# Layer 0 stores q*v once and gathers the right-hand operand when it is used

## The chip, the cores and the metric

The kernel runs on one core of a Trainium2 chip. The core has five instruction streams: TensorE (PE: matmuls, with weight loads listed as PEld), VectorE (DVE), ScalarE (ACT), GpSimd (POOL) and SyncE (SP). SP, ACT and POOL also issue DMA transfers; the packets of all transfers are moved by the same 16 DMA engines. The metric is the device time of one execution in microseconds; lower is better. A time is the median of several runs.

## The reference, cut to what matters

Four layers run on eight images of 56 x 56 pixels with 192 channels, all in float32: a gated Toeplitz layer (layer 0), window attention, an exponential-average and convolution layer, and a convolution block. The change touches layer 0 alone:

```python
q = silu(x @ q_w.T + q_b)            # 576 channels
v = silu(x @ v_w.T + v_b)
qv = q * v                           # (image, h, w, d)
o1 = toeplitz(qv along w, a1)        # o1[h, w] = sum_w' a1[w - w'] * qv[h, w']
o2 = toeplitz(qv along h, a2)        # o2[h, w] = sum_h' a2[h - h'] * qv[h', w]
out = silu(x @ p_w.T + p_b) * (o1 + o2) @ o_w.T + o_b
```

For each channel d both sums can be had in one matrix product: the left operand holds qv over (h', w) together with a1 as a matrix over (w', w), and the right operand holds a2 as a matrix over (h', h) together with qv over (w', h). The product over the 56 + 56 contraction rows gives o1 + o2 for that channel, 56 x 56 numbers over (w, h).

## The kernel before, in words

**Two steps.** Layer 0 works in two steps, and between them qv lives in DRAM. The first step (the qv step, `layer0_qv`, line 374) computes qv for one image after another; the second (the mix step, `layer0_mix`, line 523) forms the products, gates them, projects them and adds the result to x.

**DRAM tables.** The 576 channels are nine groups of 64 (NSUB = 9). Two DRAM tensors, `left` and `right`, hold rows of QR = 56 x 64 = 3584 floats (14,336 bytes). A row of `left` is one image row h of one image and one channel group: 56 pixels w by 64 channels. A row of `right` is one image column w: 56 pixels h by 64 channels. Behind the images' rows each tensor holds the rows of its Toeplitz matrix, 64 for each channel group: 56 with coefficients and 8 of zeros. `qv_row(b, s)` and `toep_row(s)` give the first row of an image's group and of a group's matrix.

**The qv step.** An image is held as 128 partitions by 1568 pixels: channels of the upper half image in partitions 0 to 63, of the lower half in 64 to 127. A pixel tile is two image rows, 112 pixels, of both halves; there are 14 for each half image (PH). For a tile, TensorE computes q and v for the 112 pixels of each half, 288 channels at a time (line 387); VectorE adds the bias (393), ScalarE applies silu (394), VectorE multiplies q by v (395) into the tile qv, of which there are three buffers. Then SP issues, for each half, one transfer into `left` (line 398) and two into `right` (403), one for each image row. All are packets of 64 floats, 256 bytes. Between tiles, lists of small steps are worked off: the building of the Toeplitz coefficients, their 112 rows and 16 rows of zeros (lines 296 and 301, issued from ACT's queue), the mask of the next layer, and the normalization of the next image, which is called after the fifth tile of the current one.

**The mix step.** Work comes in 72 blocks: eight images by nine channel groups. For a block, `layer0_block` (line 410) loads two tiles of 128 rows, lt and rt, each with one transfer on SP's queue (line 417): even rows from one table part, odd rows from another, so that Toeplitz rows and qv rows alternate and the padding rows (zero Toeplitz rows beside rows of a neighbouring block) add nothing. The pool of these tiles, `raws`, has two buffers for each, so that the load of block n + 2 waits until block n has been copied out. Copies then bring 8 or 16 channels at a time into operand form, lc on POOL and rc in turn on VectorE and ScalarE (line 425), and TensorE multiplies them, one product for each channel (433). Results are copied from PSUM to the tile o (590, 593). There are 40 such rounds an image: eight blocks have four rounds of 16 channels, the ninth has eight rounds of eight. Between rounds, parts of the previous pass's gate (projection, silu, transposes, output projection, lines 445 to 518) are worked off. The copies run two rounds ahead of the products.

**Order.** In layer 0 the framework places instructions on each engine's queue at compile time; each engine then works its queue in order and waits on semaphores. SP's queue is shared by the stores of the qv step, the loads lt and rt, the loads of x (528) and the stores of the result (538). The first two lt loads stand among the stores of the qv step; SP reached them at 400.8 and 431.0 us.

The change alters the source patterns of these loads. Before, a load of lt or rt reads

```python
bass.AP(one.tensor, one.offset, [[QR, 64], [(odd - even) * QR, 2], [1, QR]])
```

a step and a count for each level, the slowest first: 64 rows, for each the Toeplitz and the qv part, then 3584 floats.

Of the kernel before, what the change touches and what calls it, by code (L numbers as in the profile page):

```python
# [10 lines left out]
F32 = mybir.dt.float32  # L11
AF = mybir.ActivationFunctionType
ALU = mybir.AluOpType
# [5 lines left out]
NT = H * W  # L19
# [3 lines left out]
D1 = 576  # L23
# [37 lines left out]


NH = NT // 2
NTH = NH // TT
PH = NPAIR // 2

# [23 lines left out]
def kernel(ctx: ExitStack, tc: tile.TileContext, a: dict, out: bass.AP):  # L90
# [136 lines left out]
    def toeplitz_rows(psum, pool, rows):  # L227
# [145 lines left out]

    def layer0_qv(b, xn, pool, psum, w_qv, b_qv, between):

        lv, rv = (
            z[qv_row(b, 0):qv_row(b, 0) + NSUB * W].rearrange("(s h) (w d) -> s h w d", h=W, d=64) for z in (left, right)
        )
        for i in range(PH):
            qv = pool.tile([2 * W, 2, D1], F32, name="qv", bufs=3)  # L380
            for n in range(2):
                ns = slice(n * D1 // 2, (n + 1) * D1 // 2)
                ps = [psum.tile([2 * W, 2, 512], F32, name=f"qv{s}", tag="qv") for s in range(2)]
                for which in range(2):
                    for j in range(3):
                        for s in range(2):
                            nc.tensor.matmul(  # L387
                                ps[s][:, which, 0:D1 // 2], xn[64 * s:64 * s + 64, j, bass.ts(i, 2 * W)],
                                w_qv[64 * s:64 * s + 64, j, which, ns], start=(j == 0), stop=(j == 2),
                            )  # L390
                for s in range(2):
                    act = pool.tile([2 * W, 2, D1 // 2], F32, name="act", bufs=4)
                    nc.vector.tensor_tensor(act, ps[s][:, :, 0:D1 // 2], b_qv[:, :, ns], ALU.add)  # L393
                    nc.scalar.activation(act, act, AF.Silu)  # L394
                    nc.vector.tensor_tensor(qv[:, s, ns], act[:, 0], act[:, 1], ALU.mult)
            for s in range(2):
                h0 = H // 2 * s + 2 * i
                nc.sync.dma_start(
                    lv[:, h0:h0 + 2].rearrange("s h w d -> (h w) s d"),
                    qv[:, s].rearrange("t (s d) -> t s d", d=64),  # L400
                )
                for r in range(2):
                    nc.sync.dma_start(
                        rv[:, :, h0 + r].rearrange("s w d -> w s d"),
                        qv[r * W:(r + 1) * W, s].rearrange("w (s d) -> w s d", d=64),
                    )
            for step in between[i]:
                step()

    def layer0_block(b, s, raws):  # L410


        raw = [raws.tile([128, QR], F32, name=n) for n in ("lt", "rt")]
        rows_qv, rows_t = qv_row(b, s), toep_row(s)
        for t, z, even, odd in ((raw[0], left, rows_t, rows_qv), (raw[1], right, rows_qv, rows_t)):
            one = z[even:even + 64]
            nc.sync.dma_start(
                t, bass.AP(one.tensor, one.offset, [[QR, 64], [(odd - even) * QR, 2], [1, QR]]),
            )
        return raw  # L420

    def layer0_operand(copy, raw, name, bufs, d0, nu, pool):

        c = pool.tile([128, 2, 8, W], F32, name=name, bufs=bufs)
        copy(c[:, 0:nu], raw.rearrange("p (w u d) -> p u d w", u=nu, d=64 // nu)[:, :, d0:d0 + 8])  # L425
        return c

    def layer0_products(op, nu, lc, rc):
# [893 lines left out]
    with ExitStack() as st:  # L1322
        pool = st.enter_context(tc.tile_pool(reuse_waits="tile", name="qv", bufs=2))
        psum = st.enter_context(tc.tile_pool(reuse_waits="tile", name="qvp", bufs=4, space=PSUM))
        w_qv = resident("w_qv", nc.scalar, pool)
        b_qv = pool.tile([2 * W, 2, D1], F32, name="b_qv", bufs=1)
        nc.scalar.dma_start(b_qv.rearrange("p a d -> p (a d)"), a["b_qv"].partition_broadcast(2 * W))
        tz = st.enter_context(tc.tile_pool(reuse_waits="tile", name="tz", bufs=2))
        x = layer0_load(0, pool)
        xn = layer0_in(0, x, pool, psum)  # L1330
        rows, masks = [], []
        coefs, bias = toeplitz_rows(psum, tz, rows), build_bias_mask(psum, tz, masks)
        centred = layer1_weights(tz, psum)

        def pop(todo, n=1):
            for _ in range(min(n, len(todo))):
                todo.pop(0)()

        for b in range(nimg):

            between = {i: [lambda i=i: pop(rows, 2 if i % 3 == 1 else 1)] for i in range(PH)}
            if b == 0:
                for i in range(PH):
# [340 lines left out]
```

## Time and profile before

| what | us |
|---|---|
| median of three runs | 5754.3 (5746.17 to 5769.35) |
| profiled execution, its own time | 5770.6 |
| its span, first to last instruction | 5768.8 |
| qv step (28.6 to 848) | 819 |
| mix step (848 to 2053) | 1205 |
| the other layers | 3716 |
| TensorE busy in the three stretches | 731, 1084, 3365 |

The profile is of one execution. Matmuls are pipelined, so a busy TensorE is not TensorE at its peak. A group line gives the line of the kernel, the engine, the output and input names, the shape, the count, then busy time and the mean nanoseconds of one, then the idle time of the engine just before such instructions and what ended it. "q1" is the DMA queue that SP fills, "q10" the one that ACT fills; a queue line gives packets, megabytes, and the time that the packets took as a share of 16 engines' time. Where a line of digits stands, it is the busy share of the DMA engines in tenths over 40 equal slices of the window.

### The profile page before, as it was taken

The numbers are of one execution on the slowest core, as the hardware profiler recorded it, in microseconds if no ns is written. First come the engines' busy times: TensorE is split into PE (matmuls) and PEld (weight loads), VectorE is DVE, ScalarE is ACT, GpSimd is POOL, SyncE is SP. The second block draws the span as 40 slices with busy tenths as digits, with TensorE's granted clock in tenths as the row PEclk, the third lists the DMA queues.
The fourth block names the chain that finished last, engine by engine and source line by source line (L and its number), as shares of the span: only waits on it lengthen the run. The fifth ranks groups of instructions, "written<-read, shape, count | busy, mean of one in ns | idle before, by whom it ended". The sixth has DMA issues, their size and how long they took to land. (4 is left out here: it accounts for less than half of the span.)

```text
span 5768.8 us, 116138 instructions
## 1 busy us (share of the span) xinstructions
PE 5181.2 (90%) x50342; PEld 3376.1 (59%) x50342; DVE 3336.5 (58%) x4710; ACT 2169.1 (38%) x2908; POOL 1420.2 (25%) x1107
## 2 busy tenths in 40 slices
PE   6898998999899979999997989999788798999999
PEld 4568765666666645555554657676344597444444
DVE  5777774555555546566665868888778202433331
ACT  2333443333333423333332004555476400433333
POOL 2100004444444424433342013333101101100100
PEclk8999999999999989999998989999899899999999
DMA  6888986776677633222222866666687598212211
GB/s 179 204 211 216 206 182 258 264 264 258 247 262 264 222 92 82 69 75 76 69 65 76 260 235 218 227 232 209 160 232 215 222 328 295 78 62 77 76 41 26
DMA packets 721922, 1013.94 MB, mean 176 GB/s; under 512 B 486376, under 2 KB 645444, under 8 KB 694644
## 3 DMA queue, kind: packets, MB, share of 16 engines
q1 hardware_dynamic: 706352, 940.12, 52.4%
q0 software_dynamic: 8512, 40.62, 2.1%
q10 hardware_dynamic: 6548, 25.78, 1.4%
q8 instruction: 396, 6.49, 0.5%
q14 instruction: 114, 0.93, 0.0%
HBM read 676.92 MB, written 345.97 MB: 177 GB/s over the span
## 5 line engine op out<-in xcount | busy, mean ns | idle before, releaser
L387 PE MATMUL qv<-w_qv_sb,xn 64*112 64x288 f32 x5376 | 711.3, 421 | 48.6 <-DVE act L393 45.4
L425 POOL COPY lc<-lt 128x896 f32<-128x896 f32 (+1 forms) x320 | 552.5, 1751 | 640.9 <-PE op L433 543.1
L387 PEld LDWEIGHTS qv<-w_qv_sb,xn 64*112 64x112 f32 x5376 | 558.5, 182 | 195.5 <-DVE act L393 58.1
L394 ACT ACTIVATE act<-act 112x576 f32<-112x576 f32 x448 | 300.6, 683 | 466.8 <-DVE act L393 427.4
L433 PE MATMUL op<-rc,lc 128*56 128x56 f32 x9216 | 339.1, 221 | 102.1 <-POOL lc L425 64.9
L433 PEld LDWEIGHTS op<-rc,lc 128*56 128x56 f32 x9216 | 307.8, 135 | 177.9 <-POOL lc L425 103.5
L1289 PE MATMUL ph<-y,w_sb 64*128 64x392 f32 x2304 | 397.7, 497 | 6.5 <-ACT hid L1293 6.5
L1300 PE MATMUL po<-hid,w_sb 128*64 128x392 f32 x2304 | 386.3, 494 | 0.0
L393 DVE TENSOR_TENSOR act<-qv,b_qv 112x576 f32<-112x576 f32 x448 | 320.7, 752 | 92.7 <-PE qv L387 92.4
L1307 DVE TENSOR_TENSOR x<-x,z 128x392 f32<-128x392 f32 x96 | 67.0, 698 | 524.2 <-ACT z L1305 524.2
L425 ACT COPY rc<-rt 128x896 f32<-128x896 f32 (+1 forms) x160 | 256.3, 1606 | 249.7 <-PE op L433 227.2
L805 PE MATMUL qk_ps<-xr,wg 64*96 64x392 f32 x1536 | 334.2, 538 | 1.8 <-DVE xr L752 1.7
L1016 PE MATMUL cv<-zc,wt 128*128 128x224 f32 x1536 | 313.6, 356 | 24.2 <-DMA zc<-pd 24.2
L1016 PEld LDWEIGHTS cv<-zc,wt 128*128 128x128 f32 x1536 | 291.0, 190 | 67.5 <-issue 51.2
L1289 PEld LDWEIGHTS ph<-y,w_sb 64*128 64x128 f32 x2304 | 220.0, 188 | 175.9 <-issue 25.5
L445 PE MATMUL pj<-xn,w_p_sb 64*128 64x392 f32 x1536 | 309.8, 511 | 12.4 <-DVE xn L533 8.2
L1190 PE MATMUL cps<-zc,wt 128*128 128x224 f32 x1536 | 300.2, 356 | 18.2 <-DMA zc<-zd 16.8
L1190 PEld LDWEIGHTS cps<-zc,wt 128*128 128x128 f32 x1536 | 289.6, 189 | 28.7 <-issue 21.3
L466 PE MATMUL y<-pp,w_o_sb 128*64 128x392 f32 x1536 | 285.9, 501 | 4.8 <-DVE x L474 4.1
L459 DVE TENSOR_TENSOR pp<-pp,ot 128x784 f32<-128x784 f32 x128 | 124.2, 970 | 284.8 <-ACT pp L450 272.9
L1300 PEld LDWEIGHTS po<-hid,w_sb 128*64 128x64 f32 x2304 | 162.7, 137 | 213.8 <-issue 213.8
L1031 POOL TENSOR_TENSOR rows<-rows,loc 128x896 f32<-128x896 f32 x96 | 220.8, 2300 | 261.7 <-ACT rows L1027 201.9
(233 smaller groups left out, 8895.1 us busy)
## 6 DMA issues: line engine op xcount, KB each, us to landing
lt<-left SPq DMA_DIRECT2D x72, 1792.0 KB
rt<-right SPq DMA_DIRECT2D x72, 1792.0 KB
left<-qv SPq DMA_DIRECT2D x224, 252.0 KB
right<-qv SPq DMA_DIRECT2D x448, 126.0 KB
wt<-in_band_dram SPq DMA_DIRECT2D x23, 2048.0 KB
wt<-in_band_dram SPq DMA_DIRECT2D x11, 4096.0 KB
zc<-pd SPq DMA_DIRECT2D x187, 232.0 KB
pd<-pt SPq DMA_DIRECT2D x7, 5568.0 KB
```

What stands on the lines that cost most here:

```text
L387: nc.tensor.matmul(ps[s][:, which, 0:D1 // 2], xn[64 * s:64 * s + 64, j, bass.ts(i, 2 * W)], w_qv[64 * s:64 * s + 64, j, which, ns], start ...
L393: nc.vector.tensor_tensor(act, ps[s][:, :, 0:D1 // 2], b_qv[:, :, ns], ALU.add)
L394: nc.scalar.activation(act, act, AF.Silu)
L425: copy(c[:, 0:nu], raw.rearrange("p (w u d) -> p u d w", u=nu, d=64 // nu)[:, :, d0:d0 + 8])
L433: nc.tensor.matmul(op[64 * u:64 * u + W, i, :], lc[:, u, i], rc[:, u, i], start=True, stop=True)
L445: nc.tensor.matmul(ps[0:M, s, 0:TT], w_p[64 * s:64 * s + 64, j, d0:d0 + M], xn[64 * s:64 * s + 64, j, ts], start=(j == 0), stop=(j == 2),)
L466: nc.tensor.matmul(y[64 * s:64 * s + 64], w_o[0:M, c, 64 * j:64 * j + 64], pp[0:M, s], start=(c == gated[0][0]), stop=(c == gated[-1][0]),)
L805: nc.tensor.matmul(in_pairs(ps[s]), wg[64 * s:64 * s + 64, j, c0:c0 + HC], in_slots(xr[64 * s:64 * s + 64], (3 * g + j) * GW), start=(j == ...
L1016: nc.tensor.matmul(dst, wt[:, c4 + i, 128 * q:128 * q + 128], zc[:, :, c4 + i, q:q + NPAIR], start=(q == 0), stop=(q == 1),)
L1190: nc.tensor.matmul(dst.rearrange("p (b n) -> p b n", n=NPAIR), wt[:, c4 + i, q * OP:(q + 1) * OP], zc[:, :, c4 + i, q:q + NPAIR], start=(q ...
L1289: nc.tensor.matmul(ps[:, s, 0:TT], w0[64 * s:64 * s + 64, j, m * 128:(m + 1) * 128], y[64 * s:64 * s + 64, j, ts], start=(j == 0), stop=(j ...
L1300: nc.tensor.matmul(ps[64 * s:64 * s + 64], w1[:, m, 64 * j:64 * j + 64], hid[:, m, s], start=(m == 0), stop=(m == 5),)
```

## The change

Pixel tiles are now cut without regard to image rows: twelve of 120 pixels and one of 128 for each half image, 13 in place of 14 (QT). qv is stored once, to `left`, one transfer for each half; the stores to the images' rows of `right` are gone, and `right` holds the Toeplitz rows alone. The right-hand operand's qv half is gathered in the mix step out of the rows of `left`: for each column w, 56 packets of 64 floats. The rows of zeros are gone and a block has 112 rows, the first 56 of one part and the last 56 of the other. For lt this is one transfer whose source pattern lists the two parts first, then the 56 rows; for rt there are two transfers. The operand tiles lc and rc have 112 rows.

```diff
+QT = [(120 * i, 120) for i in range(12)] + [(1440, 128)]
...
-    none = dram.tile([QR], F32, name="none")
-    left, right = (dram.tile([(nimg * W + 64) * NSUB, QR], F32, name=n) for n in ("left", "right"))
+    left, right = (dram.tile([n * NSUB, QR], F32, name=z) for n, z in ((nimg * W + 64, "left"), (64, "right")))
...
-        zero = pool.tile([128, QR // 128], F32, name="zero", bufs=1)
-        nc.gpsimd.memset(zero, 0.0)
-        nc.scalar.dma_start(none.rearrange("(p n) -> p n", p=128), zero)
-        parts = [z[toep_row(0):].rearrange("(s k) n -> k s n", k=64) for z in (left, right)]
+        parts = [z[at:].rearrange("(s k) n -> k s n", k=64) for z, at in ((left, toep_row(0)), (right, 0))]
...
-        def zeros(i, k):
-            nc.scalar.dma_start(parts[i][k], none.partition_broadcast(NSUB))
-
-        rows += [lambda i=i, k=k: zeros(i, k) for i in range(2) for k in range(W, 64)]
...
     def layer0_qv(b, xn, pool, psum, w_qv, b_qv, between):
-        lv, rv = (
-            z[qv_row(b, 0):qv_row(b, 0) + NSUB * W].rearrange("(s h) (w d) -> s h w d", h=W, d=64) for z in (left, right)
-        )
-        for i in range(PH):
-            qv = pool.tile([2 * W, 2, D1], F32, name="qv", bufs=3)
+        one = left[qv_row(b, 0):qv_row(b, 0) + NSUB * W]
+        for i, (t0, M) in enumerate(QT):
+            qv = pool.tile([128, 2, D1], F32, name="qv", bufs=3)
...
-                                ps[s][:, which, 0:D1 // 2], xn[64 * s:64 * s + 64, j, bass.ts(i, 2 * W)],
+                                ps[s][0:M, which, 0:D1 // 2], xn[64 * s:64 * s + 64, j, t0:t0 + M],
...
             for s in range(2):
-                h0 = H // 2 * s + 2 * i
                 nc.sync.dma_start(
-                    lv[:, h0:h0 + 2].rearrange("s h w d -> (h w) s d"),
-                    qv[:, s].rearrange("t (s d) -> t s d", d=64),
+                    bass.AP(one.tensor, one.offset + 64 * (NH * s + t0), [[64, M], [64 * NT, NSUB], [1, 64]]),
+                    qv[0:M, s].rearrange("t (s d) -> t s d", d=64),
                 )
-                for r in range(2):
-                    nc.sync.dma_start(
-                        rv[:, :, h0 + r].rearrange("s w d -> w s d"),
-                        qv[r * W:(r + 1) * W, s].rearrange("w (s d) -> w s d", d=64),
-                    )
...
     def layer0_block(b, s, raws):
         raw = [raws.tile([128, QR], F32, name=n) for n in ("lt", "rt")]
-        rows_qv, rows_t = qv_row(b, s), toep_row(s)
-        for t, z, even, odd in ((raw[0], left, rows_t, rows_qv), (raw[1], right, rows_qv, rows_t)):
-            one = z[even:even + 64]
-            nc.sync.dma_start(
-                t, bass.AP(one.tensor, one.offset, [[QR, 64], [(odd - even) * QR, 2], [1, QR]]),
-            )
+        x = left[qv_row(b, s):qv_row(b, s) + W]
+        nc.sync.dma_start(
+            raw[0][0:2 * W], bass.AP(x.tensor, x.offset, [[(toep_row(s) - qv_row(b, s)) * QR, 2], [QR, W], [1, QR]])
+        )
+        nc.sync.dma_start(raw[1][0:W], right[64 * s:64 * s + W])
+        nc.sync.dma_start(
+            raw[1][W:2 * W].rearrange("w (h d) -> w h d", d=64), x.rearrange("h (w d) -> w h d", d=64)
+        )
         return raw

     def layer0_operand(copy, raw, name, bufs, d0, nu, pool):
-        c = pool.tile([128, 2, 8, W], F32, name=name, bufs=bufs)
-        copy(c[:, 0:nu], raw.rearrange("p (w u d) -> p u d w", u=nu, d=64 // nu)[:, :, d0:d0 + 8])
+        c = pool.tile([2 * W, 2, 8, W], F32, name=name, bufs=bufs)
+        copy(c[:, 0:nu], raw[0:2 * W].rearrange("p (w u d) -> p u d w", u=nu, d=64 // nu)[:, :, d0:d0 + 8])
         return c
...
-            between = {i: [lambda i=i: pop(rows, 2 if i % 3 == 1 else 1)] for i in range(PH)}
+            between = {i: [lambda i=i: pop(rows, 2 if i % 3 == 1 else 1)] for i in range(len(QT))}
```

Left out are the bias, activation and product lines of `layer0_qv`, which take the first M rows of their tiles, the bias tile `b_qv`, which has 128 rows in place of 112, and the loop that works off the coefficient steps, which runs over the 13 tiles.

More of the change, by code (lines that the diff above doesn't have):

```diff
@@ L374, in layer0_qv @@
     def layer0_qv(b, xn, pool, psum, w_qv, b_qv, between):
-        lv, rv = (
-            z[qv_row(b, 0):qv_row(b, 0) + NSUB * W].rearrange("(s h) (w d) -> s h w d", h=W, d=64) for z in (left, right)
-        )
-        for i in range(PH):
-            qv = pool.tile([2 * W, 2, D1], F32, name="qv", bufs=3)
+        one = left[qv_row(b, 0):qv_row(b, 0) + NSUB * W]
+        for i, (t0, M) in enumerate(QT):
+            qv = pool.tile([128, 2, D1], F32, name="qv", bufs=3)
             for n in range(2):
                 ns = slice(n * D1 // 2, (n + 1) * D1 // 2)
-                ps = [psum.tile([2 * W, 2, 512], F32, name=f"qv{s}", tag="qv") for s in range(2)]
+                ps = [psum.tile([128, 2, 512], F32, name=f"qv{s}", tag="qv") for s in range(2)]
                 for which in range(2):
@@ L391, in layer0_qv @@
                 for s in range(2):
[L392 to L395, printed above, removed]
+                    act = pool.tile([128, 2, D1 // 2], F32, name="act", bufs=4)
+                    nc.vector.tensor_tensor(act[0:M], ps[s][0:M, :, 0:D1 // 2], b_qv[0:M, :, ns], ALU.add)
+                    nc.scalar.activation(act[0:M], act[0:M], AF.Silu)
+                    nc.vector.tensor_tensor(qv[0:M, s, ns], act[0:M, 0], act[0:M, 1], ALU.mult)
             for s in range(2):
-                h0 = H // 2 * s + 2 * i
                 nc.sync.dma_start(
-                    lv[:, h0:h0 + 2].rearrange("s h w d -> (h w) s d"),
-                    qv[:, s].rearrange("t (s d) -> t s d", d=64),
-                )
-                for r in range(2):
-                    nc.sync.dma_start(
-                        rv[:, :, h0 + r].rearrange("s w d -> w s d"),
-                        qv[r * W:(r + 1) * W, s].rearrange("w (s d) -> w s d", d=64),
-                    )
+                    bass.AP(one.tensor, one.offset + 64 * (NH * s + t0), [[64, M], [64 * NT, NSUB], [1, 64]]),
+                    qv[0:M, s].rearrange("t (s d) -> t s d", d=64),
+                )
             for step in between[i]:
@@ L1325 @@
         w_qv = resident("w_qv", nc.scalar, pool)
-        b_qv = pool.tile([2 * W, 2, D1], F32, name="b_qv", bufs=1)
-        nc.scalar.dma_start(b_qv.rearrange("p a d -> p (a d)"), a["b_qv"].partition_broadcast(2 * W))
+        b_qv = pool.tile([128, 2, D1], F32, name="b_qv", bufs=1)
+        nc.scalar.dma_start(b_qv.rearrange("p a d -> p (a d)"), a["b_qv"].partition_broadcast(128))
         tz = st.enter_context(tc.tile_pool(reuse_waits="tile", name="tz", bufs=2))
@@ L1339 @@
         for b in range(nimg):
-            between = {i: [lambda i=i: pop(rows, 2 if i % 3 == 1 else 1)] for i in range(PH)}
+            between = {i: [lambda i=i: pop(rows, 2 if i % 3 == 1 else 1)] for i in range(len(QT))}
             if b == 0:
-                for i in range(PH):
+                for i in range(len(QT)):
                     between[i].insert(0, lambda: [next(coefs, None) for _ in range(2)])
```

## The prediction, made before the result was known

> **What bounds the kernel now.** I read the page first, for who is busy and how often the lines of the diff run.
>
> ```profile
> PE 5181.2 (90%) x50342; PEld 3376.1 (59%) x50342; DVE 3336.5 (58%) x4710; ACT 2169.1 (38%) x2908; POOL 1420.2 (25%) x1107
> ...
> L387 PE MATMUL qv<-w_qv_sb,xn 64*112 64x288 f32 x5376 | 711.3, 421 | 48.6 <-DVE act L393 45.4
> ...
> lt<-left SPq DMA_DIRECT2D x72, 1792.0 KB
> ```
>
> TensorE is the busy engine overall, but only layer 0 is touched, so the stretches come next: the qv step, the mix step, the untouched rest, and one steady stretch of qv.
>
> ```profile
> 28.60:848.00 819.40, 731.27 (x5514) 574.94 (x5514) 598.94 (x1124) 320.40 (x469) 42.88 (x76) 0.93 0.85 197
> 848.00:2053.00 1205.00, 1084.20 (x14932) 728.82 (x14932) 652.41 (x817) 470.02 (x467) 556.12 (x326) 0.97 0.67 249
> 2053.00:5768.80 3715.80, 3364.51 (x29896) 2071.34 (x29892) 2073.62 (x2734) 1377.18 (x1972) 811.04 (x682) 0.96 0.47 147
> ...
> 750.00:825.00 75.00, 75.00 (x622) 55.69 (x620) 60.29 (x104) 34.37 (x52) 0.00 (x0) 1.00 0.88 180
> ```
>
> The columns after the length are PE, PEld, DVE, ACT and POOL busy, granted clock, DMA share, GB/s. Undisturbed, qv is paced by TensorE (75.00 of 75 us). In the mix step TensorE is busy 1084 of 1205 us; DMA is not the pace over the whole (0.67). What the loads cost now is in the view of tile lt, and where they run in the DMA view of one image's last block.
>
> ```profile
> L425 POOL COPY lc<-lt x320: 944/1763/2862, 848.5 to 2040.9; 128x896 f32<-128x896 f32 x128, 128x448 f32<-128x448 f32 x32
> ...
>   DMA lt<-left: 62.7, 14
> ```
>
> ```profile
> DMA  5096999999950000000000000000000000979990
> ...
> q1 hardware_dynamic: 464, 5.73, 36.6%
> ```
>
> POOL waited for lt only 62.7 us in 14 places. In the second view (1700 to 1740) the engines run full for a dozen us, then idle until a buffer comes free: loads come in bursts over all engines, with slack. Last, how a transfer spreads. The packet records show one 4-byte packet per engine at the end of each transfer, so these count engines. While the Toeplitz rows are written:
>
> ```profile
> q10 hardware_dynamic: 991, 7.10, 8.6%
> ...
> left<-coef ACTq DMA_DIRECT2D x55, 126.0 KB
> ```
>
> 55 transfers of nine 14,336-byte rows are 495 packets; the other 496 are nine closings each: nine engines, not 16. The packet records give 3 engines for coef<-ct (111 outer rows). On SP's queue they hold 28,000 closings for 1,806 transfers: exactly 16 for each whose outer count is 64, 112 or 128, and 14 for each of the 448 right<-qv with 56. The count always divides the outer count.
>
> **The change part by part.**
>
> *Thirteen tiles for fourteen.* A tile is 48 matmul records (5376/112); 75 us/622 is 0.1206 us each, 5.8 us a tile. Eight tiles fewer: -46 us, on the path since TensorE paces. DVE, its cover, needs 4 x (0.752 + 0.461) = 4.9 us a tile and stays under. A weight load of 120 columns lies between 0.182 us (112, this line) and 0.188 us (128, L1289), both under a pair of matmuls; zero, at worst 2496 x 0.006 = 15 us if exposed.
>
> *Stores.* 448 SP issues of right<-qv and their 58 MB go; 224 of left<-qv become 208. Steady qv runs at DMA 0.88 with TensorE full, so nothing is waited for there; ACT's waits for left<-qv (12.2 us) are the upper bound. I take 0. The 16 zero rows on ACT's queue (0.69 us each, 11 us in image 0, where ACT is mostly idle) also go: 0, at best -11.
>
> *lt, 112 rows.* The destination still has 112 outer rows, but the source pattern now begins with the pair [.., 2], then 56 rows; before it began with 64, then the pair. If the engines divide the outer index on both sides, two engines carry everything: 56 rows each. The median packet of 14,336 bytes takes 0.535 us in the packet records: 56 x 0.535 = 30.0 us a block, where 128/16 x 0.535 = 4.3 us do now. The trace has no transfer with unequal counts below 16, so the other end is a spread by the destination's 112: 3.75 us. I take two engines: the nearest rows, 9, 56 and 111, all lost engines to their outer count, and a slice by the outer index of both sides can't be finer than 2.
>
> [...]
>
> *rt, in two pieces.* The Toeplitz half, 56 rows: 14 engines, four packets each, 4 x 0.535 = 2.1 us. The gather is 56 x 56 packets of 256 bytes, 224 on each of 14 engines. Nearest row, the same size in the other direction:
>
> ```profile
> q1 hardware_dynamic: 71655, 17.96, 87.6%
> ```
>
> 0.876 x 16 x 100 us / 71,655 = 0.0196 us a packet (725 to 825): 4.4 us. Ends: 15 ns (shortest 196-byte mask read in the packet records) gives 3.4 us, 46 ns (their median) 10.3 us.
>
> [...]
>
> *Mix step.* If the two engines also carry their share of rt, each block holds them 30.0 + 2.1 + 4.4 = 36.5 us, against 1205/72 = 16.7 us a block now. raws has two buffers: the load of block n+2 is issued when block n is copied out, at most some 19 us after it landed in the first eight blocks of an image, so a load is always queued and the ring runs on. From the third block, 70 x 36.5 = 2555. Each image's x load and two stores ride the same rings: 8 packets x 0.70 us and 24 of 6,272 bytes, about 0.24 us each: 11 x 8 = 90. The ninth block is held from 1702.4 to 1740.1 in POOL's timeline, 38 us, so the ring waits some 3.5 us: 25 for seven. Together 2670 us. Now these 70 take from the issue at 862.4 to about 1996 (the last lt is issued at 1986.3, ten us before it lands): 1134. Difference +1536. What follows the last load is the same. SP sees three issues per block for two and waits in order; it is otherwise empty there. Queued behind lt on these rings are rt and x, counted above.
>
> POOL, DVE and ACT copies are priced by the free size and keep 896 elements (112 rows for 128): 0. Matmuls keep 56 columns: 0. The cover that hid the loads, the gate work between the products, is gone at 30 us a load.
>
> *The first two lt inside qv.* SP issues them at 400.8 and 431.0, between stores. Stores behind them share the two rings.
>
> ```profile
> 425.00:450.00 25.00, 16.94 (x122) 13.44 (x122) 12.76 (x26) 8.03 (x11) 0.54 (x1) 0.90 0.99 296
> ```
>
> There TensorE already loses 8 us to one. At 30 us, less two spare qv tiles of 5.8, the loss is 18: +10 each, +20; between 0 and +44 (nothing spare).
>
> **Sum.** -46 + 20 + 1536 = +1510 us. On the profiled execution's 5770.6 that is 7281; it stood 16 above the median of 5754.3, so I predict 7265.
>
> **The rivals.**
>
> *A, lt spreads over 16 engines and the kernel is faster.* Engines 1 to 14 then carry 3.75 + 2.1 + 4.4 = 10.3 us a block, against 256/16 x 0.535 = 8.6 now and 16.7 of work. The waits for lt (62.7) grow by some 10 to 20 and the tiles give -46: about 5720, -0.6%. It decides from where a block's load fits in 16.7 us: lt on seven engines or more (112/7 x 0.535 = 8.6, plus 6.5). For it: destination 112 would allow 16. Against: the counts above.
>
> *B, lt on two engines, the pieces of rt on others.* The trace names no engine per packet. Then a block is 30.0: 70 x 6.5 = 455 less, 6810.
>
> *C, dear gather.* At 46 ns the block is 42.4: +5.9 x 70 = 413, 7680. With lt spread out it would be 16.2 us, about +5 on the eight blocks that now take some 11 us each: 5754 - 46 + 320 = 6030.
>
> **How the numbers follow.** The likeliest, two engines with rt behind lt, 0.77; B 0.08; C 0.07 with two engines and 0.02 with lt spread; A 0.06. The likeliest alone: packets at 0.586 us (1700 to 1740: 0.366 x 16 x 40 us / 400 large packets) give +3.1 x 70 = +215, and 15 ns in the gather gives -70: 7190 to 7490. The range takes in B and C: 6790 to 7690. 0.5%, about 29 us, is what a measurement of this kernel can tell (three runs spread over 23). Of A, 0.05 is faster and 0.01 within 0.5%; the other cases are slower, 0.94.
>
> **What would show it.** Right: in the mix step a DMA share near 0.28, GB/s near 95, POOL or the rc copies waiting for lt or rt about 20 us a block, lt<-left and rt<-right leading the waits, and 1,152 large lt packets fewer (16 x 72, the padding rows). The qv step: 4992 matmuls and about 790 us. Wrong: a mix step near 1205 with POOL's wait for lt under 100 us (A), waits that end on rt alone (C), or blocks 30 us apart (B). The prediction falls if lt's closings are 16 a transfer.

## The result, and the profile after

The changed kernel takes 7600.9 us (four runs, 7597.9 to 7604.6) against 5761.8 for the kernel before: 1.3195 times as long, 95% interval 1.3159 to 1.3231. Its profiled span is 7599.8 us against 5768.8. By stretches; the mix step runs from the start of the first lc copy to the start of the last o copy:

| stretch, us | before | after |
|---|---|---|
| qv step, up to the first copy | 848.5 | 834.3 |
| mix step | 1204.3 | 3051.6 |
| the other layers | 3716.0 | 3713.8 |

From the page of the changed kernel, the busy times and the costliest groups of layer 0:

```profile
PE 5418.5 (71%) x49958; PEld 3515.4 (46%) x49958; DVE 3253.4 (43%) x4646; ACT 2143.1 (28%) x2876; POOL 1367.5 (18%) x1106
...
L420 PE MATMUL op<-rc,lc 112*56 112x56 f32 x9216 | 460.6, 274 | 1437.9 <-DVE rc L412 1371.1
...
L412 POOL COPY lc<-lt 112x896 f32<-112x896 f32 (+1 forms) x320 | 499.7, 1583 | 2541.0 <-DMA lt<-left 1936.9
L412 DVE COPY rc<-rt 112x896 f32<-112x896 f32 (+1 forms) x160 | 140.1, 910 | 1676.2 <-DMA rt<-left 1660.6
...
L378 PE MATMUL qv<-w_qv_sb,xn 64*120 64x288 f32 (+1 forms) x4992 | 668.0, 425 | 37.2 <-DVE act L384 33.8
```

TensorE was 90% busy and is 71% busy. The products wait 1371 us for VectorE's copies to rc, those copies wait 1661 us for rt, and POOL waits 1937 us for lt: behind all three stand loads. The windows of the three stretches (length, then PE, PEld, DVE, ACT and POOL busy, granted clock, DMA share, GB/s):

```profile
28.60:834.00 805.40, 687.38 (x5122) 539.27 (x5120) 560.03 (x1058) 298.25 (x436) 39.14 (x71) 0.90 0.52 126
834.00:3886.00 3052.00, 1362.74 (x14930) 901.25 (x14932) 598.42 (x817) 466.05 (x467) 503.17 (x326) 0.67 0.38 88
3886.00:7599.80 3713.80, 3364.84 (x29896) 2072.18 (x29892) 2081.16 (x2734) 1375.95 (x1972) 812.25 (x682) 0.96 0.47 147
```

All of the loss lies in the mix step, where the DMA engines move 88 GB/s in place of 249 and are 0.38 busy: slow and mostly idle at once. The view of tile lt (issues with least, median and longest duration in ns; then what POOL waited for, us and times):

```profile
L400 SPq DMA_DIRECT2D lt<-left x72: 615/31996/48967, 372.9 to 3783.1; - x72
...
  DMA lt<-left: 1936.9, 70
```

and the DMA view of 18 us in which only an lt load is under way:

```profile
DMA  1211011111001111001111001111101111101111
...
q1 hardware_dynamic: 68, 0.97, 12.8%
```

12.8% is two engines of 16. The 4-byte closing packets, one for each engine that carries a transfer, say the same: SP's queue has 21,136 in the changed kernel, which comes out exactly with two for each lt, 14 for each piece of rt, 15 for a store of 120 rows and 16 for one of 128, all other transfers as in the kernel before. The issue of such a load took SP 0.5 us before; its median is now 32 us, about as long as the load moves. SP's own timeline over one block:

```profile
903.20 32.18 SPq L400 DMA_DIRECT2D lt<-left  x1
935.57 0.88 SPq L403 DMA_DIRECT2D rt<-right  x1
936.50 0.38 SPq L404 DMA_DIRECT2D rt<-left  x1
944.49 31.60 SPq L400 DMA_DIRECT2D lt<-left  x1
```

The rt loads go out only after lt's issue has ended, and the next lt follows 41.3 us after the one before. What the rt loads do when they come is in the DMA view of 936 to 948:

```profile
DMA  2009115999469948548999999999999999957122
...
q1 hardware_dynamic: 2846, 1.79, 84.3%
```

Twelve engines that had nothing to do move their shares of rt in one burst of some ten us, and then idle again.

### The profile page after: what moved, and what is told of

Same layout as the page of the kernel before. It is cut to its first block, busy times and chain, and to the rows that moved or that the text cites. A ratio compares the mean times of both kernels' runs of the same rounds, so it can differ in the third digit from the quotient of the medians.

```text
span 7599.8 us, 114683 instructions
## 1 busy us (share of the span) xinstructions
PE 5418.5 (71%) x49958; PEld 3515.4 (46%) x49958; DVE 3253.4 (43%) x4646; ACT 2143.1 (28%) x2876; POOL 1367.5 (18%) x1106
## 5 line engine op out<-in xcount | busy, mean ns | idle before, releaser
L420 PE MATMUL op<-rc,lc 112*56 112x56 f32 x9216 | 460.6, 274 | 1437.9 <-DVE rc L412 1371.1
L420 PEld LDWEIGHTS op<-rc,lc 112*56 112x56 f32 x9216 | 427.0, 185 | 1509.7 <-issue 1438.9
L412 POOL COPY lc<-lt 112x896 f32<-112x896 f32 (+1 forms) x320 | 499.7, 1583 | 2541.0 <-DMA lt<-left 1936.9
L412 ACT COPY rc<-rt 112x896 f32<-112x896 f32 (+1 forms) x160 | 254.6, 1591 | 1828.6 <-DMA rt<-left 1698.5
L378 PE MATMUL qv<-w_qv_sb,xn 64*120 64x288 f32 (+1 forms) x4992 | 668.0, 425 | 37.2 <-DVE act L384 33.8
L378 PEld LDWEIGHTS qv<-w_qv_sb,xn 64*120 64x120 f32 (+1 forms) x4992 | 523.4, 192 | 175.8 <-DVE act L384 45.5
L385 ACT ACTIVATE act<-act 120x576 f32<-120x576 f32 (+1 forms) x416 | 279.6, 683 | 470.4 <-DVE act L384 432.4
L384 DVE TENSOR_TENSOR act<-qv,b_qv 120x576 f32<-120x576 f32 (+1 forms) x416 | 297.6, 751 | 96.7 <-PE qv L378 96.6
L432 PEld LDWEIGHTS pj<-xn,w_p_sb 64*128 64x128 f32 x1536 | 172.0, 206 | 349.2 <-ACT pp L437 217.5
L1021 DVE TENSOR_TENSOR_SCAN sums<-dec,rows 64x896 f32<-64x896 f32 x96 | 279.3, 2910 | 1.3
```

Source lines behind the costliest of these rows:

```text
L378: nc.tensor.matmul(ps[s][0:M, which, 0:D1 // 2], xn[64 * s:64 * s + 64, j, t0:t0 + M], w_qv[64 * s:64 * s + 64, j, which, ns], start=(j == ...
L384: nc.vector.tensor_tensor(act[0:M], ps[s][0:M, :, 0:D1 // 2], b_qv[0:M, :, ns], ALU.add)
L385: nc.scalar.activation(act[0:M], act[0:M], AF.Silu)
L412: copy(c[:, 0:nu], raw[0:2 * W].rearrange("p (w u d) -> p u d w", u=nu, d=64 // nu)[:, :, d0:d0 + 8])
L420: nc.tensor.matmul(op[64 * u:64 * u + W, i, :], lc[:, u, i], rc[:, u, i], start=True, stop=True)
L432: nc.tensor.matmul(ps[0:M, s, 0:TT], w_p[64 * s:64 * s + 64, j, d0:d0 + M], xn[64 * s:64 * s + 64, j, ts], start=(j == 0), stop=(j == 2),)
```

## The experiments

Each is compared with runs of the kernel before on the same chip. "Large packet" is a row of 14,336 bytes, "small" one of 256 bytes; their times are means over the packet records of the mix step (median where said); the small packets of the stores and of the copies inside DRAM are those of the qv step.

| kernel | time, us | ratio to before, 95% | mix step, us | large packet, us | small, ns |
|---|---|---|---|---|---|
| before | 5754 to 5765 | 1 | 1204.3 | 0.584 (median 0.535) | 19.6 (stores) |
| after | 7600.9 | 1.3159 to 1.3231 | 3051.6 | 0.746 | 32 |
| lt as two transfers | 6115.0 | 1.0580 to 1.0625 | 1638.6 | 1.027 | 33 |
| lt on three engines | 6835.2 | one run | 2339.0 | 0.821 | 31 |
| before, lt on two engines | 7905.8 | one run | 3282.2 | 0.842 | - |
| no gather | 6039.2 | 1.0456 to 1.0494 | 1539.0 | 1.008 | - |
| before, in halves | 6120.2 | 1.0592 to 1.0648 | 1544.5 | 1.070 | - |
| halves on two queues | 6230.4 | 1.0771 to 1.0837 | 1734.2 | 1.002 and 0.942 | 31 |
| 112 rows, alternating | 6064.8 | 1.0501 to 1.0542 | 1557.5 | 1.015 | 32 |
| 128 rows, gather | 5958.6 | 1.0342 to 1.0373 | 1459.3 | 0.604 (median 0.535) | 22 |
| before, program order | 5852.5 | 1.0143 to 1.0175 | 1301.3 | 0.570 (median 0.535) | - |
| 128 rows, gather, program order | 5831.9 | 1.0106 to 1.0136 | 1349.3 | 0.605 (median 0.535) | 22 |
| lt as two transfers, program order | 6121.7 | 1.0602 to 1.0637 | 1643.6 | 1.028 | 33 |
| right copied inside DRAM | 5738.3 | 0.9943 to 0.9976 | 1241.9 | 0.583 (median 0.535) | 18 |

**Is it the two engines?** The theory of the prediction: lt's source pattern begins with a level of two, so two engines carry the whole block. Three kernels test it: take the level away, put it into the kernel before, and change two into three.

```diff
-        nc.sync.dma_start(
-            raw[0][0:2 * W], bass.AP(x.tensor, x.offset, [[(toep_row(s) - qv_row(b, s)) * QR, 2], [QR, W], [1, QR]])
-        )
+        nc.sync.dma_start(raw[0][0:W], x)
+        nc.sync.dma_start(raw[0][W:2 * W], left[toep_row(s):toep_row(s) + W])
```

> The changed kernel with lt loaded by two transfers of 56 rows (outer count 56 on both sides, as the two parts of rt) in place of one with outer count 2. Theory (two engines carry lt): 8 packets of 0.54 us on each of 14 engines instead of 56 on each of two; lt, rt and the gather then hold an engine for about 11 us a block, under the 16.7 us of work, so the mix step comes back from 3052 us to 1205 to 1270 and the whole to 5700 to 5800 us. Rival (the gather of 256-byte packets is what costs): lt is a small part, the mix step stays over 2500 us and the whole over 7000.

The same for the kernel before, the other way round:

```diff
-        for t, z, even, odd in ((raw[0], left, rows_t, rows_qv), (raw[1], right, rows_qv, rows_t)):
...
+        nc.sync.dma_start(
+            raw[0], bass.AP(one.tensor, one.offset, [[(rows_t - rows_qv) * QR, 2], [QR, 64], [1, QR]]),
+        )
+        for r, at in ((0, rows_t), (64, rows_qv)):
+            nc.sync.dma_start(raw[1][r:r + 64], right[at:at + 64])
```

> The kernel before with lt loaded by one transfer whose source lists the two parts first and then 64 rows (outer count 2), rt by two transfers of 64 rows; 14 pixel tiles, both stores and the zero rows as before, no gather. Theory: 64 packets of 0.54 us on two engines are 34.6 us, with rt's eight packets 39 us a block; mix step about 70 x 39 + 115 = 2845 and the whole 7350 to 7550 us, though nothing else of the change is in it. Rival (the gather or the 112 rows cost it): near the kernel before, 5740 to 5850 us.

And three engines, by cutting each half of lt into 51 rows (three divides 51) and five:

```diff
+        for r, at in ((0, qv_row(b, s)), (W, toep_row(s))):
+            nc.sync.dma_start(raw[0][r:r + 51], left[at:at + 51])
+            nc.sync.dma_start(raw[0][r + 51:r + W], left[at + 51:at + W])
```

> The changed kernel with each half of lt loaded as 51 rows and 5 rows. If an engine count must divide the outer count (51 = 3 x 17, 5), three engines carry nearly all: 2 x (17 + 1) = 36 packets, 19.5 us, with rt 2.2 and the gather 4.4 a block of 26 us, plus about 2 where rt's burst meets it: mix step 2000 to 2250, whole 6450 to 6800 us. Rival (any split into two or more transfers cures it, because it was the unequal shapes of the two sides that cost): the same as with two transfers of 56 rows, 5700 to 5800 us.

Measured: 6115 us without the level of two, 7906 us with it in the kernel before, which has no gather and all its stores, and 6835 us with three engines. All three lie above the ranges given in advance, by 315, 356 and 35 us. The DMA view of a stretch of lt in the kernel before with that pattern (3002 to 3050):

```profile
DMA  1111111111111111111111111111111111111111
...
q1 hardware_dynamic: 186, 2.57, 12.6%
```

and of the kernel with three engines (1500 to 1700):

```profile
DMA  6988999411289311289511279621269712168912
...
q1 hardware_dynamic: 20508, 23.67, 54.2%
```

The closing packets on SP's queue come out exactly with 14 engines for each half of lt in the first kernel (23,008 in all), two for lt in the second (28,144), and three and five for its pieces in the third (22,144). The two-engine pattern is enough for the loss: the second kernel's rt also comes in halves, but the kernel before with both tiles in halves, further down, takes 6120 us. One engine more gives back 713 of 3052 us of the mix step. The cause is shown from both sides. But without it the kernel is still 6% behind the kernel before, where the prediction's rival A had put a spread load at 5720.

**What holds the other 6%? First the gather.** In the kernel with lt as two transfers, the gather is replaced by a contiguous load of the same 56 rows; the exchange of rows and columns is left out.

```diff
-        nc.sync.dma_start(
-            raw[1][W:2 * W].rearrange("w (h d) -> w h d", d=64), x.rearrange("h (w d) -> w h d", d=64)
-        )
+        nc.sync.dma_start(raw[1][W:2 * W], x)
```

> The kernel with lt in two transfers of 56 rows, and the gather of 256-byte packets replaced by a load of the same 56 rows as they lie, 14,336 bytes a packet: it leaves out the exchange of rows and columns in the right-hand qv, so it computes another sum; same bytes, same work elsewhere. Theory: the gather costs an engine 4.4 to 9 us a block where the large packets cost 2.2, but the blocks have slack, so the whole is 0 to 60 us under the kernel with the gather. Rival (the gather is the bottleneck once lt is spread): more than 150 us under it.

6039 us against 6115: without the 3136 small packets a block the kernel is 76 us faster, a fifth of what is missing, and TensorE's order of work, of which more below, differs between the two as well. The large packets still take 1.008 us where the kernel before has 0.584, so the transfers themselves are slow.

**Then where the rows land.** The kernel before, its tables, stores and 14 tiles as they were, loads lt and rt as two halves, rows for partitions 0 to 63 and for 64 to 127, in place of alternating rows:

```diff
-            nc.sync.dma_start(
-                t, bass.AP(one.tensor, one.offset, [[QR, 64], [(odd - even) * QR, 2], [1, QR]]),
-            )
+            nc.sync.dma_start(t[0:64], z[first:first + 64])
+            nc.sync.dma_start(t[64:128], z[second:second + 64])
```

> The kernel before with lt and rt each loaded by two transfers of 64 rows to partitions 0 to 63 and 64 to 127, in place of one transfer of 64 x 2 rows to all 128; same bytes, same 16 engines by outer count, no gather, 14 pixel tiles. Theory (a transfer to half of the partitions runs at half the rate: in the last runs its 14,336-byte packets took 1.0 to 1.1 us where those of the 128-row transfers took 0.54): 16 packets of 1.07 us, 17 us a block where 8.6 were, mix step 1205 to some 1550, whole 6050 to 6200 us. Rival (the 56 rows or the 14 engines cost it): packets stay at 0.54 us and the whole at 5740 to 5800.

6120 us, large packets a median of 1.104 us, about twice 0.535: the same rows, bytes and engines (64 rows on 16 engines), in half of the partitions at a time, at half the rate. Two queues might have let the two halves overlap:

```diff
-        nc.sync.dma_start(raw[0][W:2 * W], left[toep_row(s):toep_row(s) + W])
+        nc.scalar.dma_start(raw[0][W:2 * W], left[toep_row(s):toep_row(s) + W])
...
-        nc.sync.dma_start(
+        nc.scalar.dma_start(
             raw[1][W:2 * W].rearrange("w (h d) -> w h d", d=64), x.rearrange("h (w d) -> w h d", d=64)
```

> The kernel with lt in two transfers of 56 rows (6115 us), with the second half of lt and the gather issued from ACT's queue, so that transfers to the lower and the upper partitions are under way together. Theory (each half of the partitions has its own limit, and one queue serves the halves one after the other): large packets come down toward 0.54 us, a block toward 11 to 14 us, whole 5690 to 5850 us. Rival (the rate is lost by splitting as such, or ACT's waits for buffers cost as much as is won): 6000 us or more, packets still at 1.0 us.

They did not: 0.94 to 1.00 us a packet, and 6230 us in all. ACT, which had copies of rc to do, now spent 164 us of the mix step on issues (22.3 us on one lt half), and the rc copies waited 632 us for the gather, against 304 with one queue; which of the two made the loss is not shown. Next, the changed kernel's parts in alternating partitions, lt again as one transfer with the 56 rows as the outer level:

```diff
-            raw[0][0:2 * W], bass.AP(x.tensor, x.offset, [[(toep_row(s) - qv_row(b, s)) * QR, 2], [QR, W], [1, QR]])
+            raw[0][0:2 * W], bass.AP(x.tensor, x.offset, [[QR, W], [(toep_row(s) - qv_row(b, s)) * QR, 2], [1, QR]])
...
+        even, odd = raw[1][0:2 * W].rearrange("(k r) n -> r k n", r=2)[0], raw[1][0:2 * W].rearrange("(k r) n -> r k n", r=2)[1]
+        nc.sync.dma_start(even, right[64 * s:64 * s + W])
+        nc.sync.dma_start(odd.rearrange("w (h d) -> w h d", d=64), x.rearrange("h (w d) -> w h d", d=64))
```

> The changed kernel with the two parts of lt and rt in alternate partitions: lt by one transfer whose source lists 56 rows first and then the two parts (outer counts 56 and 112: 14 engines), the Toeplitz half of rt to the even and the gather to the odd partitions, so every transfer touches lower and upper partitions. Theory (half of the partitions, half the rate): the halves are no longer served one after the other, packets under 1.0 us, whole 5720 to 6000 us. Rival (the split to 14 engines with neighbouring rows on one engine is what costs, wherever the rows go): packets stay at 1.0 to 1.1 us and the whole at 6050 to 6150.

6065 us, large packets still 1.015 us, and 1.02 where no small packet is near. And the same with the padding rows given back, 64 rows a part, so that every transfer has 16 engines:

```diff
+        nc.sync.dma_start(raw[0], bass.AP(x.tensor, x.offset, [[QR, 64], [far * QR, 2], [1, QR]]))
+        even, odd = (raw[1].rearrange("(k r) n -> r k n", r=2)[r] for r in range(2))
+        nc.sync.dma_start(even, right[64 * s:64 * s + 64])
+        nc.sync.dma_start(
+            odd.rearrange("w (h d) -> w h d", d=64), bass.AP(x.tensor, x.offset, [[64, 64], [QR, W], [1, 64]])
+        )
```

> The changed kernel with blocks of 128 rows again and its two parts in alternate partitions: lt by one transfer of 64 x 2 rows as before, the Toeplitz half of rt (64 rows, zero rows restored) to the even and the gather (64 columns, the last 8 unused) to the odd partitions; 13 pixel tiles, qv stored once. Differs from the interleaved 112-row kernel (6065 us) in 64 rows for 56. Theory (transfers whose rows divide by 64 give each engine its own part of the partitions; 56 rows make engines meet, whichever partitions they go to): large packets back at 0.54 to 0.6 us, 256-byte packets near 20 ns, a block 4.3 + 2.1 + 4.3 = 10.7 us, mix step 1205 to 1280; with the qv step 60 us shorter than before the whole is 5680 to 5780 us. Rival (it is splitting rt into a part and a gather, or loading alternate partitions, that costs): packets stay at 1.0 us and 31 ns, the whole at 6000 to 6100.

The packets are back at a median of 0.535 us and 22 ns, and 14% more bytes take 98 us less of the mix step than 112 alternating rows do. The whole still missed its range (5680 to 5780) by 179 us. So the half rate was measured in two ways: with half of the partitions (in halves, a median of 1.104 us) and with 56 rows a part on 14 engines, even over nearly all partitions (1.044). Why 14 engines cost as much as half the partitions, these runs don't say: from the alternating kernel to this one the rows, the engines and the partitions change together, and the packet records name no engine, so that engines meeting at the destination, the theory above, is argued and not shown. It is a rate of many engines at once: in the changed kernel the two engines that come last carry the same 56-row pieces at 0.538 us a row and 15.8 ns a small packet.

**The rest of it is order.** With its packets back at that rate the 128-row kernel still has a mix step of 1459 us, 255 above the kernel before, and POOL hardly waits for loads. From the view of its tile lt, what POOL waited for:

```profile
  PE op L427: 913.2, 112
  DMA lt<-left: 1.4, 3
```

Here TensorE holds the copies up. The framework had placed the gate's work elsewhere: the order in which TensorE works one image's mix step (the fourth) is, with the number of matmuls in a row (op: products; pj, ot, y: gate), from the trace:

```
before               ... op96 pj12 ot1 op32 ot13 op32 pj12 ot14 op31 y1 op1 y23 op32 pj12 ot14 ...
128 rows, gather     ... pj10 op128 pj26 op128 ot28 y16 ot2 y8 ot11 pj1 ot1 pj11 ot14 y16 pj2 y2 op128 ...
the same, pr. order  ... op32 pj12 ot14 op32 pj12 ot14 op32 y24 op64 pj12 ot14 op32 pj12 ot14 op32 y24 ...
```

In the second the gate comes in lumps, and the products eight rounds at a time (elsewhere in this image sixteen); while a lump of gate work runs, the buffers of lc and rc don't come free. That the loads alone can change the order is shown by the kernel before in halves, which differs from the kernel before in nothing else. The changed kernel, the kernel before in halves and both alternating kernels share this bunched order (all but four of 14,929 records agree). Lt as two transfers has a third order, in longer lumps, with up to 24 rounds of products in a row. To take the order out of the comparison, three kernels keep the mix step's instructions on TensorE, VectorE and ScalarE as the code issues them; POOL's order was the same in all. Their sequences are then identical from the first product to the last.

```diff
         psum = st.enter_context(tc.tile_pool(reuse_waits="tile", name="mixp", bufs=2, space=PSUM))
+        st.enter_context(tc.manual_schedule(engines=IN_ORDER))
```

> The kernel before, with the instructions of TensorE, VectorE and ScalarE in the mix step kept in the order in which the code issues them; nothing else is changed. It is the control for the next two runs, which have exactly this order on all four engines, and so differ from it by their loads and by the 13 tiles alone. What the written order itself costs is unknown: the gate pieces stand between the rounds as the lists of the code have them, which is the even spread, so the mix step should lie between 1204 us (nothing lost) and 1459 us (the bunched order of the 128-row gather kernel). Total 5750 to 6020.

> The 128-row kernel with the gather (lt as one transfer, rt as 64 Toeplitz rows to even and the gather to odd partitions), with the same fixed order of instructions in the mix step as the control. Theory order: that kernel's mix step of 1459 us against 1204 comes from gate work that the compiler bunched; with the order fixed its mix step is within 40 us of the control's, and the total is 20 to 60 us below the control's (the 13 tiles). Theory transfers: a third transfer a block and 3584 small packets cost the 217 to 255 us themselves, whatever the order; then its mix step is over 200 us above the control's.

> The changed kernel with lt as two 56-row transfers (large packets at 1.03 us, 256-byte packets at 33 ns), in the same fixed order. A block then holds each of 14 engines 8 x 1.03 + 4 x 1.03 + 224 x 0.033 = 19.8 us, against 16.7 us of work a block in the kernel before: 72 x 19.8 = 1426, less the early blocks and with the x loads about 1430 to 1500. Theory half rate: the mix step stays 1430 to 1640, 150 us or more above the 128-row kernel in the same order. Theory order: packets are slow but hidden, and its mix step is within 50 us of the 128-row kernel's.

The windows of the three mix steps, first the control (the kernel before's loads), then the 128-row gather, then lt as two transfers:

```profile
848.00:2149.00 1301.00, 1085.31 (x14926) 749.06 (x14927) 606.25 (x817) 460.94 (x466) 595.25 (x325) 0.91 0.61 230
```

```profile
782.00:2131.00 1349.00, 1092.42 (x14930) 754.04 (x14932) 604.24 (x816) 457.95 (x465) 568.13 (x325) 0.89 0.75 222
```

```profile
782.00:2426.00 1644.00, 1129.98 (x14931) 774.12 (x14932) 597.60 (x816) 457.36 (x467) 546.38 (x326) 0.83 0.83 162
```

In one and the same order the gather costs 48 us (theory "order" had allowed 40, theory "transfers" wanted over 200), and the half rate another 294 (1644 is the top of what that theory had allowed). Fixing the order took 110 us from the 128-row kernel and nothing from the one at half rate (1643.6 against 1638.6): there the DMA engines, 0.83 busy where loads on 14 of 16 can fill 0.875, are the pace, whatever TensorE's order. From the views of tile rt, what the rc copies waited for in the 128-row kernel and in the one at half rate, both in program order:

```profile
  DMA rt<-left: 387.8, 61
```

```profile
  DMA rt<-left: 967.3, 110
```

The mix steps can now be laid end to end:

| step from one kernel to the next | mix step, us |
|---|---|
| before, 1204.3; its work in program order | +97.0 |
| rt as Toeplitz rows plus a gather, 128 rows | +48.0 |
| 112 rows in halves, 14 engines (half rate) | +294.3 |
| the framework's order again | -5.0 |
| lt on two engines | +1413.0 |
| after | 3051.6 |

The first line is the price of a written order; the framework's bunched order costs still more at full rate (1459), and at half rate neither shows. Of the change's 1847 us, 1413 are the two engines, and most of the rest is the half rate. Steps taken in another sequence would share these parts out differently.

**A version that is faster than both.** The shorter qv step can be had without the loads' losses: 13 tiles, qv stored once, and the image rows of `right` filled from `left` by copies inside DRAM, one block after each of nine tiles of the next image, the last image's after the step. Both tables keep their zero rows, and the mix step's loads are the kernel before's.

```diff
+        def across(b, s):
+            z, y = (t[qv_row(b, s):qv_row(b, s) + W] for t in (left, right))
+            nc.sync.dma_start(y.rearrange("w (h d) -> w h d", d=64), z.rearrange("h (w d) -> w h d", d=64))
...
+            for i in range(9):
+                between[i + 2].append(lambda: pop(moves))
             layer0_qv(b, xn, pool, psum, w_qv, b_qv, between)
+            moves += [lambda b=b, s=s: across(b, s) for s in range(NSUB)]
```

> Loads, padding and both tables as in the kernel before, but 13 pixel tiles, qv stored once, and right filled from left by DRAM-to-DRAM copies of 256-byte packets, one block after each of nine pixel tiles of the next image; those of the last image after the qv step. Theory (the change's gain is the shorter qv step, 4992 matmuls for 5376 and fewer stores from SBUF; its loss is in the mix step's loads): mix step back at about 1205 to 1230, qv step 780 to 830 if a copied packet costs an engine about 20 to 25 ns, whole 5680 to 5780. Rival (the gather costs its 256-byte packets wherever it stands): the qv step becomes bound by DMA, over 880 us, and the whole over 5800.

5738.3 us against 5759.1, 0.4% less, ratio 0.9959 (0.9943 to 0.9976). Its windows:

```profile
28.60:792.00 763.40, 681.73 (x5124) 531.74 (x5120) 558.46 (x1058) 298.38 (x436) 40.57 (x74) 0.92 0.83 203
792.00:2034.00 1242.00, 1093.44 (x14926) 732.97 (x14927) 654.29 (x817) 469.11 (x466) 551.11 (x326) 0.96 0.67 247
```

The qv step is 56 us shorter and the mix step 38 longer, though its loads run at the old rate. The trace puts most of the 38 on the last image's nine copies. From SP's timeline, and from TensorE's:

```profile
800.37 28.82 SPq L1336 DMA_DIRECT2D right<-left  x9
829.29 3.02 SPq L521 DMA_DIRECT2D x<-in_x_dram  x1
832.42 0.56 SPq L410 DMA_DIRECT2D lt<-left  x1
```

```profile
843.25 4.29 PE L438 MATMUL pj<-xn,w_p_sb 64*128 64x392 f32 x12 [29.37 <-DVE xn L526]
```

The copies stand on SP's queue ahead of the mix step's first load of x and of the third lt; TensorE is idle for 29.4 us meanwhile, and POOL waits 32.7 us for that lt. From the 1,024th product to the 3,600th the kernel is 28 us behind the kernel before; the last ten come later, and their cause is open.

## Why the prediction was right, and where it was off

The forecast of 7265 was 336 us short of 7600.9. The mechanism held and one term was mis-sized. The likeliest case's own range (7190 to 7490) missed the measured time; that the whole range (6790 to 7690) holds it is owed to the room left for rival C, whose dear gather did not come, and that is luck.

**Two engines for lt: right.** Two closing packets for each lt, a DMA share of 12.8% while lt is alone, and 7906, 6835 and 6115 us for the same pattern elsewhere, for three engines and for 14. That the source's two would count against the destination's 112 was the author's inference: the trace of the kernel before has no transfer with unequal counts below 16. In the changed kernel two against 112 gave two engines.

**The block: 36.5 predicted, 41.0 measured; this is the term that was mis-sized.** A block has 30 closing packets (2 for lt, 14 for each piece of rt). 24 come in bunches, from the twelve engines without lt; six come singly, and their order gives the parts of the block on the two engines (us from the start of the span):

```
                 lt ends   Toeplitz rows end   gather ends   next lt ends
one engine        929.7         931.9             935.4          970.0
the other         931.5         933.7             937.2          972.1
```

The Toeplitz rows take 2.2 us (2.1 predicted) and the gather 3.5 (4.4, range from 3.4), 15.8 ns a packet, below the 19.6 of the stores. It is lt that was mis-sized: 35.2 us on average over 43 blocks, not 56 x 0.535 = 30.0. Alone its packets take a median of 0.539 us (948 to 968), 30.2 for 56, but in the burst of rt the large packets on all engines take from 0.54 to 1.49 us, and lt loses some five us in every block. The 70 blocks' 4.5 us are +315, nearly all of the miss of the mix step (3051.6 measured, 1204.3 + 1536 = 2740 predicted: +311). The 90 us for the x loads and stores and the 25 for the ninth block fit in the sum; neither was measured by itself, and the 90 counts the 6,272-byte packets at 0.24 us, where the mix step of the kernel before has a median of 0.485.

**Thirteen tiles, -46: right.** TensorE's busy time in the qv step fell from 731.3 to 687.4, by 43.9. **Stores, 0: too little.** With lt as two transfers the qv step has 66.4 us without TensorE (750.4 - 684.0) where the kernel before has 88.1. Its window:

```profile
28.60:779.00 750.40, 683.97 (x5124) 543.35 (x5120) 559.62 (x1058) 299.01 (x436) 40.36 (x73) 0.93 0.57 135
```

No run parts the stores from the zero rows; the 128-row gather kernel, which writes zero rows again, has 77.8, so that perhaps half of the gain is theirs. **The first two lt, +20, between 0 and 44: too little.** In the changed kernel that idle time is 118.0 (805.4 - 687.4), 52 more than with lt as two transfers. That is over the 44 of its range. The last two misses partly cancel, by luck: the step came out 14 us shorter, predicted 26.

**Costed at nothing: right.** The copies keep their rate (a median of 1.67 us on POOL against 1.76, of 1.74 on ScalarE against 1.75), and the other layers changed by 2 us.

**The rivals.** A fell, and its price was wrong as well: with lt spread over 14 engines the kernel takes 6115, not 5720. The prediction gave 56 and 112 rows the 0.535 us that the trace shows for 64 pairs of rows on 16 engines; on 14 they take 1.0 to 1.1. And it let the order of the work stay as it was, which it did not. B fell: blocks are 41 us apart, and the two engines carry rt behind lt. C fell: a small packet takes 32 ns on average, not 46, and most of that is on engines that have time.

Half of the partitions at a time went at about half the rate in the kernel before in halves (a median of 1.104 us against 0.535), but 112 alternating partitions went at a median of 1.044, so that no run shows half of the partitions to be the whole reason. The two engines that set the pace carried rt's halves at 0.538 us a row, and it is in the burst of the other twelve that large packets have a median of 1.02.

**What was to be seen.** DMA share 0.38 and 88 GB/s (0.28 and 95 forecast; the large packets' mean of 0.746 us in place of 0.535 counts as busy time); POOL's wait for lt 27.7 us a block (about 20); 4992 matmuls, a step of 805 us (about 790).

## What to carry to other kernels

Count the engines that carry a transfer when the outer level of its pattern changes: outer levels of two, of 51 and five, and of 56 had two, three and five, and 14 engines here, and gave 7601, 6835 and 6115 us for the same rows. Rows that look like padding can be what keeps a load at 16 engines and full rate: 128 rows went at a median of 0.535 us a packet where 112 went at 1.044. And before a small loss is put down to transfers, compare the order in which the engines do the work: 110 us of the 128-row kernel's mix step were order.

## What the runs showed of the hardware that was not expected

- In the changed kernel the issue of an lt on two engines held SP for a median of 32 us, against 0.5 before, and what stood behind it on SP waited, while 14 engines had nothing to move. In the kernel before with lt on two engines the same issue had a median of 0.53 us, so that two engines alone are not shown to be the reason.
- The lt packets of the two engines, 0.54 us alone, lost some five us a block where the other engines had a burst of some ten us: in it large packets have a median of 1.02 us.
- With 56 rows a part on 14 engines large packets took a median of 1.044 us even where the partitions alternate; with 64 rows on 16 engines in the same pattern they took 0.535, and a small packet 22 ns against 32.
- TensorE's granted clock was lower where TensorE idled between loads: 0.97 in the mix step before, 0.67 after, with a product's mean record at 274 ns against 221. The products waited 1438 us for their operands, so that the clock did not set the pace.
- Copies from DRAM to DRAM in 256-byte packets took 18 to 19 ns each, no more than the stores they replace (19.6), and beside TensorE's work.
